# Grouped 3x3 convolution: weights as integers, images as two float32r parts, general path behind a branch

## The chip, the cores and the metric

The kernel runs on one core of one Trainium2 chip. Times are device microseconds (us) of that core. A row of the trace comes from one execution that the hardware profiler recorded; the median comes from three executions without it.

## What is computed

Each image is normalised over groups of four channels, convolved with one of five quantised weight sets, and added to itself. The reference, cut to that:

```python
def _L0_conv_ref(x, U):                 # N = 5, 128 channels in and out, 3x3, padding 1
    beta = jnp.max(U)
    alpha = jnp.min(U)
    s1 = (beta - alpha) / RES_DENOS[0]          # RES_DENOS = (3.0, 5.0)
    v1 = s1 * _ste_floor(U / s1)
    s2 = s1 / RES_DENOS[1]
    v2 = s2 * _ste_floor((U - v1) / s2)
    w = (v1 + v2).reshape(OUT_CH * N, IN_CH, K, K)
    B, C, H, W = x.shape
    xb = x.reshape(B // N, N * C, H, W)
    act = jax.lax.conv_general_dilated(xb, w, ..., feature_group_count=N)
    ...
x = x + _L0_conv_ref(_gn(x), L0_conv_U)  # x: (160, 128, 32, 32) float32; _gn: 32 groups, eps 1e-5
```

A weight is v1 + v2 = s2 * (5 * k1 + k2), where k1 and k2 are the two floors, small integers.

## The kernel before

Channels lie on the 128 partitions. Image i uses set i % 5, and the images are taken set by set: 8 chunks of 4 images for each of 5 sets, 40 chunks, 160 images. SP loads a chunk of 2 MB (`load`, L165) three chunks ahead into one of four `xt` buffers, and ScalarE's queue stores it from the same buffer when its last image is done (L238).

**One image** (`conv`, L204): nine taps, each as two matrix multiplications of 128 x 128 weights with half an image (16 rows of 32, read with a row step of 34 from the padded image `pad`), 18 multiplications into one of three pairs of PSUM banks `pc`. Then VectorE adds `pc` to the image in `xt` (L220): the eviction.

**One chunk's normalisation** (`normalise`, L171) runs while the chunk before it is convolved. VectorE takes statistics of half images (L177), joins them (L178); TensorE averages the means over a group (L181) with `gavg`; VectorE makes `dv` from it in four small steps (L183 to L187); TensorE averages `dv` (L188); VectorE adds eps (L190), GpSimd takes the power -1/2 (L192), and VectorE writes the four normalised images into `pad` (L195). The two small multiplications L181 and L188 stand in TensorE's queue between those of the images.

**One weight set** (`make_weights`, L142): 17 VectorE steps over 128 x 1152 numbers (`floor_div`, L130, twice, and three more), nine transposes on TensorE (L161), three copies to SBUF on ScalarE (L162). Set 0 is made at the start, with the step sizes s1 and s2 from the range of all weights (L91 to L128); a later set is made while the set before it is convolved. All weights and images are float32.

The tile framework sets each engine's order of instructions when the program is built; engines wait for each other by semaphores, and each engine works through its own list in order.

## Time and profile before

| | |
|---|---|
| median of 3 runs | 2566.12 us (2565.94 to 2566.95) |
| profiled execution, first to last instruction (span) | 2564.2 us |
| median less span | 1.9 us |
| TensorE busy with multiplications | 2500.8 us (98%) |
| VectorE busy | 664.1 us (26%) |
| ScalarE busy | 8.5 us |
| GpSimd busy | 52.4 us |
| HBM, read and written | 67 GB/s over the span |

The page counts TensorE's multiplications (PE) and its weight loads (PEld) apart, since they overlap. A float32 multiplication of the program is two records in the trace, each with a weight load of its own: 160 images x 18 multiplications are 2880, and the page has 5760. A record's duration runs until its results are written, so that neighbours overlap: their spacing, and not their duration, is what they cost.

### The profile page before, as it was taken

What the parts mean: (1) busy time and instruction counts of PE and PEld (TensorE: products, weight loads), DVE (VectorE), ACT (ScalarE), POOL (GpSimd) and SP (SyncE); (2) the same over time, 40 slices, a digit from 0 to 9 for tenths busy, and PEclk for the clock granted to TensorE, in tenths of its full rate; (3) what the DMA queues carried; (4) which work ended last, traced back from release to release, by engine and by line L of the source; (5) the groups of instructions that cost most, each with busy time, mean ns of one, the idle gap of its engine ahead of it and who ended that gap; (6) DMA issues with size and microseconds to landing.
All of it is one profiled execution on the core that took longest, in us unless ns stands there. A gap on an engine that the chain in (4) does not pass through costs nothing.

```text
span 2564.2 us, 13452 instructions
## 1 busy us (share of the span) xinstructions
PE 2500.8 (98%) x5965; PEld 1115.1 (43%) x5965; DVE 664.1 (26%) x1113; ACT 8.5 (0%) x16; POOL 52.4 (2%) x59
## 2 busy tenths in 40 slices
PE   1999999999999999999999999999999999999998
PEld 0444444444444444444444444444444444444443
DVE  8542222222522222224222222222222222222110
ACT  0000000000000000000000000000000000000000
POOL 2000000000000000000000000000000000000000
PEclk9999999999999999999999999999999999999999
DMA  4012121111111111111111111111111111111110
GB/s 177 22 64 78 68 78 78 73 66 66 66 66 66 66 66 66 66 66 66 66 66 66 66 66 66 66 66 66 66 66 66 66 66 66 66 66 70 45 45 38
DMA packets 43019, 171.60 MB, mean 67 GB/s; under 512 B 1360, under 2 KB 1360, under 8 KB 42960
## 3 DMA queue, kind: packets, MB, share of 16 engines
q1 hardware_dynamic: 21120, 83.89, 8.8%
q10 hardware_dynamic: 21840, 86.84, 8.2%
q8 instruction: 47, 0.77, 0.1%
q14 instruction: 12, 0.10, 0.0%
HBM read 86.84 MB, written 83.89 MB: 67 GB/s over the span
## 4 chain that ended last, share of the span: by engine, by line
PE 97%; DVE 2%; DMA 1%; ACTq 0%; ACT 0%; issue 0%
PE pc L212 97%; DMA u<-in_L_conv_U_dram 1%; DVE st L177 0%; PE pt L161 0%; PE pg L181 0%; PE pg L188 0%; DVE pad L195 0%; DVE tt L137 0%; DVE tt L138 0%; DVE tt L136 0%; DVE wq L140 0%; DVE tt L139 0%; ACTq L62 0%; DVE nn L134 0%; DVE wq L153 0%; DVE ext L93 0%
## 5 line engine op out<-in xcount | busy, mean ns | idle before, releaser
L212 PE MATMUL pc<-pad,wt 128*128 128x512 f32 x5760 | 2493.6, 593 | 0.0
L212 PEld LDWEIGHTS pc<-pad,wt 128*128 128x128 f32 x5760 | 1084.7, 190 | 1340.1 <-issue 1340.1
L220 DVE TENSOR_TENSOR xt<-xt,pc 128x1024 f32<-128x1024 f32 x160 | 195.4, 1221 | 1785.2 <-PE pc L212 1785.2
L177 DVE BATCH_NORM_STATS2 st<-xt 128x6 f32<-128x512 f32 x320 | 199.8, 663 | 2.8 <-DMA xt<-in_x_dram 2.8
L195 DVE TENSOR_SCALAR pad<-xt,gm,rstd 128x1024 f32<-128x1024 f32 x160 | 119.5, 809 | 46.3 <-POOL rstd L192 46.3
L192 POOL TENSOR_TENSOR rstd<-ve,mhalf 128x4 f32<-128x4 f32 x40 | 42.1, 1053 | 2403.2 <-DVE ve L190 2393.1
L181 PE MATMUL pg<-mv,gavg 128*128 128x4 f32 x80 | 11.8, 218 | 43.1 <-DVE mv L178 43.1
L181 PEld LDWEIGHTS pg<-mv,gavg 128*128 128x128 f32 x80 | 15.4, 196 | 61.4 <-issue 44.1
L178 DVE BATCH_NORM_AGGREGATE mv<-st 128x2 f32<-128x12 f32 x160 | 31.2, 195 | 1.2
L188 PEld LDWEIGHTS pg<-dv,gavg 128*128 128x128 f32 x80 | 15.4, 196 | 26.6 <-DVE dv L187 17.5
L188 PE MATMUL pg<-dv,gavg 128*128 128x4 f32 x80 | 11.8, 218 | 8.2 <-DVE dv L187 8.2
L190 DVE TENSOR_SCALAR ve<-pg 128x4 f32<-128x4 f32 x40 | 6.5, 161 | 39.3 <-PE pg L188 39.3
L140 DVE TENSOR_TENSOR wq<-nn,tt 128x1152 f32<-128x1152 f32 x10 | 13.5, 1353 | 5.2 <-PE pt L161 5.1
L139 DVE TENSOR_TENSOR tt<-tt,nn 128x1152 f32<-128x1152 f32 x10 | 13.5, 1349 | 0.2
L161 PE MATMUL pt<-ident,wq 128*128 128x128 f32 x45 | 9.4, 323 | 3.4 <-DVE wq L153 2.7
L162 ACT COPY wt<-pt 128x512 f32<-128x512 f32 (+1 forms) x15 | 7.2, 478 | 1658.7 <-PE pt L161 1658.7
L161 PEld LDWEIGHTS pt<-ident,wq 128*128 128x128 f32 x45 | 7.0, 200 | 11.5 <-ACT wt L162 6.8
L93 DVE TENSOR_REDUCE ext<-u 128x1 f32<-128x1152 f32 x5 | 6.8, 1353 | 7.0 <-DMA u<-in_L_conv_U_dram 6.8
L87 POOL MEMSET pad<- 128x1156 f32 x8 | 8.1, 1061 | 0.0
L135 DVE TENSOR_SCALAR nn<-nn 128x1152 f32<-128x1152 f32 x10 | 7.5, 753 | 0.1
L153 DVE SCALAR_TENSOR_TENSOR wq<-wq,s,v 128x1152 f32<-128x1152 f32 x5 | 7.1, 1419 | 0.1
L137 DVE SCALAR_TENSOR_TENSOR tt<-nn,s2lo,tt 128x1152 f32<-128x1152 f32 x5 | 7.1, 1419 | 0.1
(44 smaller groups left out, 93.0 us busy)
## 6 DMA issues: line engine op xcount, KB each, us to landing
xt<-in_x_dram SPq DMA_DIRECT2D x40, 2048.0 KB, 7.4
out_dram<-xt ACTq DMA_DIRECT2D x40, 2048.0 KB, 6.4
u<-in_L_conv_U_dram ACTq DMA_DIRECT2D x5, 576.0 KB, 10.2
```

Of the source, the lines that this page charges most:

```text
L87: nc.gpsimd.memset(pad, 0.0)
L139: nc.vector.tensor_tensor(t, t, n, ALU.is_lt)
L140: nc.vector.tensor_sub(k, n, t)
L161: nc.tensor.transpose(pt[:, k, :], wq3[:, :, t0 + k], ident)
L177: nc.vector.bn_stats(st[:, h, :], xt[:, j, h * HALF : (h + 1) * HALF])
L178: nc.vector.bn_aggr(mv[:, j, :], st)
L181: nc.tensor.matmul(pg[:, 0, :], gavg2, mv[:, :, 0], start=True, stop=True)
L188: nc.tensor.matmul(pg[:, 1, :], gavg2, dv, start=True, stop=True)
L192: nc.gpsimd.tensor_tensor(rstd, ve, mhalf, ALU.pow)
L195: nc.vector.tensor_scalar(pad[:, 1 : H + 1, 1 : W + 1], xt[:, j, :].rearrange("p (h w) -> p h w", w=W), gm[:, j : j + 1], rstd[:, j : j + ...
L212: nc.tensor.matmul(pc[:, h, :].rearrange("p (h w) -> p h w", w=W), wt[:, tap, :], pad[:, r0 : r0 + HROWS, kw : kw + W], start=(tap == 0), ...
L220: nc.vector.tensor_add(xj, xj, pc)
```

## The change

The weights that TensorE gets are the integers 5 * k1 + k2 (`make_weights`, L274 of the kernel after), of type float32r. The eviction multiplies by the step size s2 and adds the image in one instruction (L332). An image is normalised into a plain buffer `z` by VectorE (L302), copied to float32r by ScalarE (`hi`, L311), and VectorE writes the rest z - hi as float32r (`lo`, L312). Each tap is then four multiplications: `hi` and `lo`, each for two halves of the image, with the same weights. There are six pairs of padded images in place of eight images, and an image is split two images ahead of its convolution rather than four at a time (`split`). Statistics are as before, in a function of their own (`group_statistics`).

At the end every engine reads a flag (`far`, L165), which was made from the range of the weights at the start, and branches: for weights whose magnitude is over 256 times their range, the whole work is done once more in float32, image by image, in loops (`general_path`, L156). With these inputs the branch skips that.

The diff, cut to its core:

```diff
+MM = mybir.dt.float32r
...
+        self.s2z = col("s2z")
+        nc.vector.tensor_scalar_mul(self.s2z, self.s2, 1.0 / SCALE)
...
+        big, far = col("big"), col("far")
+        self.far = col("fari", I32)
+        nc.vector.tensor_reduce(big, extg, AX.X, ALU.max)
+        nc.vector.scalar_tensor_tensor(far, span, WIDEST, big, ALU.mult, ALU.is_lt)
+        nc.vector.tensor_copy(self.far, far)
...
+def general_path(tc, keep, steps, x, u, out):
...
+    far = nc.values_load(steps.far[0:1, 0:1], min_val=0, max_val=1)
+    with tc.If(far > 0), ExitStack() as ctx:
...
     def make_weights(n):
...
-        nc.vector.scalar_tensor_tensor(wq, wq, s2, v1, ALU.mult, ALU.add)
-
-        wt = const.tile([P, TAPS, C], F32, tag=f"wt{n}", name=f"wt{n}")
...
+        k1, k2, _ = steps.quantise(qpool, us[n], n)
+        nc.vector.scalar_tensor_tensor(k2, k1, 5.0, k2, ALU.mult, ALU.add)
+        wt = const.tile([P, TAPS, C], MM, tag=f"wt{n}", name=f"wt{n}")
...
-        for j in range(NB):
-            pad = pads[(g % 2) * NB + j]
-            nc.vector.tensor_scalar(
-                pad[:, 1 : H + 1, 1 : W + 1],
...
+    def split(g, j, xt, gm, rstd):
+
+        hi, lo = pads[(g * NB + j) % N_PADS]
+        z = zpool.tile([P, H, W], F32, tag="z", name=f"z{g}_{j}")
+        nc.vector.tensor_scalar(
+            z,
...
+        hi_in = hi[:, 1 : H + 1, 1 : W + 1]
+        nc.scalar.copy(hi_in, z)
+        nc.vector.tensor_sub(lo[:, 1 : H + 1, 1 : W + 1], z, hi_in.bitcast(F32))
...
-            for h in range(2):
-                r0 = h * HROWS + kh
-                nc.tensor.matmul(
...
+            for part in range(2):
+                for h in range(2):
+                    r0 = h * HROWS + kh
+                    nc.tensor.matmul(
+                        pc[:, h, :].rearrange("p (h w) -> p h w", w=W),
+                        wt[:, tap, :],
+                        pair[part][:, r0 : r0 + HROWS, kw : kw + W],
...
-        nc.vector.tensor_add(xj, xj, pc)
+        nc.vector.scalar_tensor_tensor(xj, pc, steps.s2z, xj, ALU.mult, ALU.add)
```

**TensorE, around the two small multiplications of a chunk.** Before, they stand in the third image of the chunk ahead; `pc` is an image's result, `pg` theirs:

```order
L212 MATMUL pc_1_376<-pad_107,wt_187 128x512 x18
L181 MATMUL pg_413<-mv_396,gavg 128x4
L212 MATMUL pc_2_430<-pad_109,wt_187 128x512 x3
L188 MATMUL pg_413<-dv_417,gavg 128x4
L212 MATMUL pc_2_430<-pad_109,wt_187 128x512 x15
```

After, in the second image, for a chunk behind the first ones:

```order
L139 MATMUL pg_1167<-mv_1150,gavg 128x4
L324 MATMUL pc_1_1184<-hi_123,wt_210 128x512 x2
L324 MATMUL pc_1_1184<-lo_125,wt_210 128x512 x2
L324 MATMUL pc_1_1184<-hi_123,wt_210 128x512 x2
L324 MATMUL pc_1_1184<-lo_125,wt_210 128x512 x2
L324 MATMUL pc_1_1184<-hi_123,wt_210 128x512 x2
L146 MATMUL pg_1167<-dv_1171,gavg 128x4
```

Between the two stand three multiplications (six records) before, and ten after.

**VectorE, the same place** (behind the eviction whose image ends just ahead of the first small one). Before:

```order
L220 TENSOR_TENSOR xt_257<-xt_257,pc_1_647 128x1024
L183 COPY gm_686<-pg_684 128x4
L185 TENSOR_TENSOR dv_688<-mv_667,gm_686 128x4
L186 TENSOR_TENSOR dv_688<-dv_688 128x4
L187 TENSOR_TENSOR dv_688<-dv_688,mv_667 128x4
L190 TENSOR_SCALAR ve_693<-pg_684 128x4
L195 TENSOR_SCALAR pad_97<-xt_374,gm_686,rstd_695 128x32x32
```

After:

```order
L332 SCALAR_TENSOR_TENSOR xt_507<-pc_0_1110,s2z,xt_507 128x1024
L141 COPY gm_1169<-pg_1167 128x4
L143 TENSOR_TENSOR dv_1171<-mv_1150,gm_1169 128x4
L144 TENSOR_TENSOR dv_1171<-dv_1171 128x4
L145 TENSOR_TENSOR dv_1171<-dv_1171,mv_1150 128x4
L148 TENSOR_SCALAR ve_1176<-pg_1167 128x4
L302 TENSOR_SCALAR z_0_1222<-xt_746,gm_1169,rstd_1178 128x1024
L302 TENSOR_SCALAR z_1_1264<-xt_746,gm_1169,rstd_1178 128x1024
L312 TENSOR_TENSOR lo_113<-z_0_1222,hi_111 128x32x32
L312 TENSOR_TENSOR lo_117<-z_1_1264,hi_115 128x32x32
```

The chain from the eviction to `dv` is the same; the subtractions that make `lo` are added behind it.

**VectorE, the same chain for chunk 2, early in the program, after the change**, where the quantiser of set 2 (`k`, `v`, `u`) stands between its small steps:

```order
L332 SCALAR_TENSOR_TENSOR xt_184<-pc_0_469,s2z,xt_184 128x1024
L141 COPY gm_528<-pg_526 128x4
L93 TENSOR_TENSOR k_2_2271<-nn_2269,tt_2270 128x1152
L143 TENSOR_TENSOR dv_530<-mv_509,gm_528 128x4
L104 TENSOR_SCALAR v_2_2273<-k_2_2271,s_146 128x1152
L144 TENSOR_TENSOR dv_530<-dv_530 128x4
L105 TENSOR_TENSOR u_86<-u_86,v_2_2273 128x1152
L145 TENSOR_TENSOR dv_530<-dv_530,mv_509 128x4
```

There the chain has three large steps more than in the later chunks.

## Rows read from the trace of the kernel before

**Rows 1.** Page: busy time of the engines; and the chain that ended last.

```profile
PE 2500.8 (98%) x5965; PEld 1115.1 (43%) x5965; DVE 664.1 (26%) x1113; ACT 8.5 (0%) x16; POOL 52.4 (2%) x59
...
PE 97%; DVE 2%; DMA 1%; ACTq 0%; ACT 0%; issue 0%
```

**Rows 2.** Groups by line: tiles, shapes, count | busy us, mean ns | idle before.

```profile
L212 PE MATMUL pc<-pad,wt 128*128 128x512 f32 x5760 | 2493.6, 593 | 0.0
L212 PEld LDWEIGHTS pc<-pad,wt 128*128 128x128 f32 x5760 | 1084.7, 190 | 1340.1 <-issue 1340.1
```

**Rows 3.** Pieces of the chain in order of time: start us, us, what.

```profile
279.39 2.68 PE pc L212 x6
282.19 59.35 PE pc L212 x138
341.66 2.68 PE pc L212 x6
```

**Rows 4.** Timeline around one chunk's small multiplications: start us, us, engine, instruction.

```profile
341.38 0.28 PE L181 MATMUL pg<-mv,gavg 128*128 128x4 f32 x2
...
341.52 2.82 PE L212 MATMUL pc<-pad,wt 128*128 128x512 f32 x6
341.58 1.22 DVE L220 TENSOR_TENSOR xt<-xt,pc 128x1024 f32<-128x1024 f32 x1 [9.03 <-PE pc L212]
342.04 0.19 PEld L212 LDWEIGHTS pc<-pad,wt 128*128 128x128 f32 x1 [0.24 <-issue]
...
342.72 0.15 DVE L183 COPY gm<-pg 128x4 f32<-128x4 f32 x1
...
343.30 0.16 DVE L187 TENSOR_TENSOR dv<-dv,mv 128x4 f32<-128x4 f32 x1
```

**Rows 5.** Timeline of TensorE and ScalarE at the transposes of set 1.

```profile
169.28 0.62 PE L161 MATMUL pt<-ident,wq 128*128 128x128 f32 x4
169.28 0.42 PEld L161 LDWEIGHTS pt<-ident,wq 128*128 128x128 f32 x3 [0.24 <-issue]
...
171.33 0.58 ACT L162 COPY wt<-pt 128x512 f32<-128x512 f32 x1 [0.81 <-PE pt L161]
...
172.19 3.17 PE L212 MATMUL pc<-pad,wt 128*128 128x512 f32 x7
172.39 0.27 ACT L162 COPY wt<-pt 128x128 f32<-128x128 f32 x1 [0.47 <-PE pt L161]
```

**Rows 6.** Timeline of the start: first load issued and seen, last quantiser step, images begin.

```profile
0.79 2.77 ACTq L62 DMA_DIRECT2D u<-in_L_conv_U_dram  x5
...
6.41 1.35 DVE L93 TENSOR_REDUCE ext<-u 128x1 f32<-128x1152 f32 x1 [6.41 <-DMA u<-in_L_conv_U_dram]
...
54.91 1.42 DVE L153 SCALAR_TENSOR_TENSOR wq<-wq,s,v 128x1152 f32<-128x1152 f32 x1
...
61.01 29.41 PE L212 MATMUL pc<-pad,wt 128*128 128x512 f32 x67
```

**Rows 7.** Groups by line, VectorE: as rows 2.

```profile
L177 DVE BATCH_NORM_STATS2 st<-xt 128x6 f32<-128x512 f32 x320 | 199.8, 663 | 2.8 <-DMA xt<-in_x_dram 2.8
L220 DVE TENSOR_TENSOR xt<-xt,pc 128x1024 f32<-128x1024 f32 x160 | 195.4, 1221 | 1785.2 <-PE pc L212 1785.2
L195 DVE TENSOR_SCALAR pad<-xt,gm,rstd 128x1024 f32<-128x1024 f32 x160 | 119.5, 809 | 46.3 <-POOL rstd L192 46.3
...
L139 DVE TENSOR_TENSOR tt<-tt,nn 128x1152 f32<-128x1152 f32 x10 | 13.5, 1349 | 0.2
...
L137 DVE SCALAR_TENSOR_TENSOR tt<-nn,s2lo,tt 128x1152 f32<-128x1152 f32 x5 | 7.1, 1419 | 0.1
```

**Rows 8.** Busy us (x instructions) in one chunk's period, then clock, DMA share, GB/s.

```profile
311.00:373.27 62.27, 62.27 (x150) 27.71 (x149) 13.76 (x26) 0.00 (x0) 1.01 (x1) 1.00 0.17 68
```

**Rows 9.** The same, from the last eviction's start to the end.

```profile
2555.54:2564.20 8.66, 0.00 (x0) 0.00 (x0) 1.22 (x1) 0.00 (x0) 0.00 (x0) 0.79 0.59 242
```

## The prediction

> **What bounds the kernel now.** I read the page's busy shares first, then its chain, then the pieces of the chain in order of time. TensorE is busy for 98% of the span and makes up 97% of the chain [rows 1]; nearly all of it is one line, the image multiplications, in 5760 records that never waited (idle before: 0.0) [rows 2]. Their duration, 593 ns, is not what they cost, since they overlap. The chain gives the spacing: 138 records in 59.35 us, 430.07 ns each [rows 3]. [...] Everything else is hidden behind that: a chunk takes 62.27 us, in which VectorE works 13.76 us and ScalarE not at all [rows 8]. The rest of the time is a start of 61.0 us, in which VectorE makes the first weights [rows 6], and an end of 8.7 us with the last eviction and the last store [rows 9].

> The sum for the kernel as it is: start 61.0; 5760 x 0.43007 = 2477.2; small multiplications, 62.27 - 144 x 0.43007 = 0.34 per chunk, times 39 = 13.3; transposes of four later sets, 172.19 - 169.28 = 2.91 us less the four image records between them (1.72) = 1.2 each, 4.8 in all [rows 5]; end 8.7. That is 2565.0 against a span of 2564.2. The median lies 1.9 us above the span, and I carry that along.

> **The change part by part.**

> *Multiplications.* A tap had two multiplications of two records, 4 x 430 = 1720 ns; it gets four float32r ones. Their number, 160 x 36 = 5760, is the number of records before, so the question is what one record costs. No float32r record stands in this trace. From below: one stream of 512 columns is half of 430.07, 215.0 ns; from above: 860 ns, if the type changes nothing. I take one stream plus the whole 3.4 ns, 216.7 ns, because the split into `hi` and `lo` parts with integer weights has a purpose only where a factor is cut to the digits of one stream. 5760 x 0.2167 = 1248.4.

> *Weight loads.* There are as many as before, 5760, each 190 ns long [rows 2], now in half the time. A load starts with the multiplication ahead of it and is over long before that ends (0.19 of 0.43 us [rows 4]); of 216.7 ns it would still leave 27. Pairs of load and multiplication can follow closer than that: the two 4-column ones take 0.14 us together, 70 ns a pair [rows 4], and transposes of 128 columns, where three loads take 0.42 us, are (0.42 - 0.19) / 2 = 115 ns apart [rows 5]. So I count the loads at nothing; the cover is the running multiplication, and without it one costs up to 70 ns, 403 us in all.

> [...]

> *Start.* VectorE's list up to the end of set 0's weights has the same quantiser steps and the same 19 half-image statistics as before. New are six `lo` subtractions, two more `z`, and four tiny steps. A float32 two-input step of 1152 is 1.349 us [rows 7], for 1024 that is 1.22, and the next starts 0.08 before its end (341.58 + 1.22 against 342.72 [rows 4]), so 1.14: six are 6.8. Two `z` at 0.809 - 0.08 are 1.5; the tiny ones 0.5. Sum 8.8, which nothing hides: TensorE starts its images at 61.0 + 8.8 = 69.8. ScalarE's copies (below) lie beside other steps there.

> *Per chunk.* TensorE's period becomes 144 x 0.2167 + 0.34 = 31.5 us. VectorE has its 12.5 (13.76 less the fifth eviction in that window), four `lo` (4.9) and four evictions that multiply too (0.07 more each, by 1.419 against 1.349 [rows 7]): 17.7 of 31.5. ScalarE copies four images: 512 columns take 0.58 and 128 take 0.27 [rows 5], so 1024 about 1.0, 4 us per chunk. Loads and stores move 68 GB/s in this period [rows 8] and would move 135; the end alone has 242 [rows 9]. All covered by TensorE.

> *The wait for `dv`.* The second small multiplication stood six records, 2.6 us, behind the first; now ten, 2.17 us. VectorE's chain to `dv` takes from 341.38 to 343.46, 2.08 us [rows 4], and 0.07 more with the new eviction: 2.15, while the load of the second one wants to start at 0.14 + 9 x 0.2167 = 2.09. It falls short by a little in each chunk; behind the waiting load stand all further image multiplications. From 0 to 0.2 us; I take 0.1 for 35 chunks, 3.5.

> *Early chunks.* The scheduler has put the quantiser of sets 1 to 3 between VectorE's work for chunks 1 to 4, and TensorE now comes past twice as early. Laying VectorE's list end to end with the times above (quantiser steps at 1.33, 1.27 and 0.7): 48 us from the end of set 0's weights, 65.2, to chunk 2's `dv`, 113.3, where TensorE wants it at 69.8 + 5 x 7.8 + 5.8 = 114.6; another 35 to chunk 3's, 148.5, wanted at 147.5; chunk 4's within 1 us. One more such place is at set 3 and 4. I take 4 us, with 0 to 12 as bounds. PSUM's three pairs let evictions be up to two images late, and they are not.

> *Branch.* Five engines read a flag and jump. TensorE, GpSimd and SP do it while the last store (7 us) is under way. No row shows a jump; a trip to memory bounds it, 0.79 to 6.41 [rows 6], 5.6 us, and below it is nothing. I take 1. Transposes and small multiplications stay float32.

> **Sum:** 69.8 + 1248.4 + 13.3 + 4.8 + 3.5 + 4 + 8.7 + 1.9 + 1 = 1355.4, about 1355 us, 47% below 2566.

> **The rivals.**
> *Loads shown.* Loads that a two-stream record covers are not covered by one stream (a load may need the running record's first stream over before it takes effect). For it: the transposes, 115 ns apart where a single stream of 128 columns is 53. Against it: the 27 ns left, and 70 ns pairs. Price 5760 x 0.070 = 403, less the waits (7.5), which then vanish: about 1750.
> *Two streams per float32r record.* A 4-byte operand passes in two streams whatever its name. [...] Then 5760 x 0.43007 = 2477.2 stays, the waits vanish, and start and branch remain: 2577, slower by 0.4%. It decides from a spacing of 428 ns on, where the saving no longer pays for the 9.8 us of start and branch.
> *The type changes nothing.* float32r is run as float32, four streams: 860 ns, 4954 for the multiplications, about 5050. Only the type's name in the program stands against it; no row.

> **How the numbers follow.** The forecast has 0.84: the split is pointless otherwise. Loads shown 0.07, two streams 0.06, nothing changed 0.03. The forecast's own bounds are 1338 (215.0 ns, no waits) and 1372 (waits and branch at their upper ends). No bound stands between a hidden load and a shown one, so I stretch the upper end by a fifth of a load, 14 ns, 80 us, that could show: 1336 to 1430 leaves out the rivals and the forecast's tails. A difference of 0.2% (5 us) is about what can be measured. Faster by more: the first two cases, 0.91. Slower: two streams and nothing changed, 0.09, of which 0.02 falls within 0.2%, as that case lies near its edge.

> **What would show it.** Right: image multiplications in 5760 records at a spacing near 217 ns, about 380 ns long; loads still 190 ns and each beginning with the multiplication ahead; a chunk's period of 31.6 us; TensorE's images starting near 70 us; VectorE busy some 800 us, waiting for TensorE; waits of TensorE for `dv` of some us in chunks 2 to 4 and 11 and of 0.1 elsewhere. Wrong: a spacing near 285 (loads shown), 430 (two streams), or twice as many records; a chunk's period set by VectorE or ScalarE; more than 6 us between the last store's landing and the end.

## The result and the profile after

The changed kernel takes 1505.62 us (median of 4 runs, 1504.94 to 1506.34) against 2566.53 us before: a ratio of 0.5866, with a 95% interval of 0.5858 to 0.5875. It takes 41% less time. The prediction had the direction, but its 1355 us and the upper end of its range, 1430, are too low. The profiled execution spans 1504.2 us.

The page, as [rows 1]: TensorE still makes the chain, 95% of it; VectorE has 846 us in place of 664, ScalarE 170 in place of 8.5.

```profile
PE 1430.8 (95%) x5965; PEld 1119.2 (74%) x5965; DVE 846.3 (56%) x1277; ACT 169.7 (11%) x176; POOL 57.1 (4%) x63
...
PE 95%; DVE 3%; DMA 1%; ACTq 0%; ACT 0%; issue 0%
```

The groups by line (tiles, shapes, count | busy us, mean ns | idle before), as [rows 2]. The number of records is the same, 5760, so a float32r multiplication is one record; it lasts 408 ns in place of 593. Loads still take 190 ns, and multiplications wait for nothing.

```profile
L324 PE MATMUL pc<-hi,wt 128*128 128x512 f32 x2880 | 940.8, 408 | 0.0
L324 PE MATMUL pc<-lo,wt 128*128 128x512 f32 x2880 | 940.4, 408 | 0.0
L324 PEld LDWEIGHTS pc<-lo,wt 128*128 128x128 f32 x2880 | 544.8, 190 | 150.8 <-issue 0.2
```

The pieces of the chain (start us, us, what), as [rows 3]; the first is the first chunk of all, the others one later chunk. 134 records take 32.72 us: 244.2 ns each, where 430.07 was the spacing before and 216.7 the forecast.

```profile
69.46 44.60 PE pc L324 x177
...
934.13 0.12 PE pg L139 x2
934.25 2.55 PE pc L324 x10
936.80 0.12 PE pg L146 x2
936.92 32.72 PE pc L324 x134
```

The busy time of the engines (PE, PEld, DVE, ACT, POOL, with instructions), then clock, DMA share and GB/s, for one chunk's period and for the end, as [rows 8, 9]. VectorE and ScalarE work 18.36 and 4.10 of 35.51 us, so nothing but TensorE sets the period.

```profile
224.44:259.95 35.51, 35.51 (x150) 27.78 (x150) 18.36 (x29) 4.10 (x4) 1.01 (x1) 1.00 0.30 122
1494.23:1504.20 9.97, 0.00 (x0) 0.00 (x0) 1.28 (x1) 0.00 (x0) 0.00 (x0) 0.60 0.53 215
```

The timeline around a chunk's two small multiplications, as [rows 4]: `dv` ends at 1363.36, the load of the second small multiplication begins at 1363.64. TensorE no longer waits there.

```profile
1361.42 1.28 DVE L332 SCALAR_TENSOR_TENSOR xt<-pc,s2z,xt 128x1024 f32<-128x1024 f32 x1 [7.49 <-PE pc L324]
...
1363.20 0.16 DVE L145 TENSOR_TENSOR dv<-dv,mv 128x4 f32<-128x4 f32 x1
...
1363.64 0.43 PEld L146 LDWEIGHTS pg<-dv,gavg 128*128 128x128 f32 x2
1363.88 0.28 PE L146 MATMUL pg<-dv,gavg 128*128 128x4 f32 x2
```

So one term holds the miss, 27.5 ns in each of 5760 multiplications, 158 us; waits that did not come take 7.5 us of it back. The experiments ask where these nanoseconds are. Two places of the same trace narrow it before any run. One is the last image, behind the eviction of the image before it, where TensorE is the only engine at work (busy times, clock, DMA share and GB/s below) and 24 records, from 1487.21 to 1493.06, take 5.85 us, 243.8 ns each. So it is not contention with other engines.

```profile
1486.80:1494.20 7.40, 7.39 (x31) 5.42 (x29) 0.00 (x0) 0.00 (x0) 0.00 (x0) 1.00 0.01 2
```

```profile
1487.21 0.65 PE L324 MATMUL pc<-hi,wt 128*128 128x512 f32 x2
...
1493.06 0.65 PE L324 MATMUL pc<-hi,wt 128*128 128x512 f32 x2
```

The other is the first image, ahead of 72.25 us, where the records come in pairs 0.85 us apart:

```profile
69.69 1.05 PE L324 MATMUL pc<-hi,wt 128*128 128x512 f32 x2
...
70.54 1.05 PE L324 MATMUL pc<-lo,wt 128*128 128x512 f32 x2
```

That is 426.5 ns each, 0.833 ns a column. The busy-time view prints a granted clock of 1.00 here too, but the trace's first entry of a granted clock is at 72.88 us, where the spacing falls to 244; so the lower level is read from the spacing. The same 0.83 ns a column stands in e4 below at a granted clock of 0.50. My estimate from these two places is half as much at 1.00: 213.3 ns for 512 columns by themselves, 0.417 each; the 0.417 and 106.7 ns in the expectations agree with it. What is missing seems to show only when the columns pass faster than 0.833 ns each; e4 and e17 below test that.

### The profile page after: what moved, and what is told of

Read it like the earlier page. It is cut to its first block, busy times and chain, and to the rows that moved or that the text cites. A ratio compares the mean times of both kernels' runs of the same rounds, so it can differ in the third digit from the quotient of the medians.

```text
span 1504.2 us, 14064 instructions
## 1 busy us (share of the span) xinstructions
PE 1430.8 (95%) x5965; PEld 1119.2 (74%) x5965; DVE 846.3 (56%) x1277; ACT 169.7 (11%) x176; POOL 57.1 (4%) x63
## 4 chain that ended last, share of the span: by engine, by line
PE 95%; DVE 3%; DMA 1%; ACTq 0%; ACT 0%; issue 0%
PE pc L324 94%; DMA u<-in_L_conv_U_dram 1%; DVE st L135 1%; DVE lo L312 0%; PE pt L284 0%; PE pg L139 0%; PE pg L146 0%; DVE z L302 0%; DVE tt L89 0%; DVE tt L91 0%; DVE tt L90 0%; DVE tt L92 0%; DVE k L93 0%; ACTq L252 0%; DVE nn L87 0%; DVE nn L88 0%
## 5 line engine op out<-in xcount | busy, mean ns | idle before, releaser
L324 PE MATMUL pc<-hi,wt 128*128 128x512 f32 x2880 | 940.8, 408 | 0.0
L324 PE MATMUL pc<-lo,wt 128*128 128x512 f32 x2880 | 940.4, 408 | 0.0
L324 PEld LDWEIGHTS pc<-lo,wt 128*128 128x128 f32 x2880 | 544.8, 190 | 150.8 <-issue 0.2
L324 PEld LDWEIGHTS pc<-hi,wt 128*128 128x128 f32 x2880 | 543.6, 190 | 149.7
L332 DVE SCALAR_TENSOR_TENSOR xt<-pc,s2z,xt 128x1024 f32<-128x1024 f32 x160 | 204.8, 1280 | 543.7 <-PE pc L324 543.7
L311 ACT CAST hi<-z 128x1024 fp32r<-128x1024 f32 x160 | 161.2, 1053 | 1236.5 <-DVE z L302 1219.9
L312 DVE TENSOR_TENSOR lo<-z,hi 128x1024 fp32r<-128x1024 f32 x160 | 189.2, 1223 | 16.6 <-ACT hi L311 16.6
L302 DVE TENSOR_SCALAR z<-xt,gm,rstd 128x1024 f32<-128x1024 f32 x160 | 123.2, 810 | 44.6 <-POOL rstd L150 44.6
L284 PE MATMUL pt<-ident,k 128*128 128x128 f32 x45 | 8.7, 308 | 28.3 <-DVE k L277 27.7
L93 DVE TENSOR_TENSOR k<-nn,tt 128x1152 f32<-128x1152 f32 x10 | 13.5, 1355 | 2.7 <-PE pt L284 2.6
L39 DVE TENSOR_REDUCE ext<-u 128x1 f32<-128x1152 f32 x5 | 6.8, 1353 | 7.1 <-DMA u<-in_L_conv_U_dram 7.1
```

The lines of the kernel that those rows point to most:

```text
L284: nc.tensor.transpose(pt[:, k, :], k3[:, :, t0 + k], ident)
L302: nc.vector.tensor_scalar(z, xt[:, j, :].rearrange("p (h w) -> p h w", w=W), gm[:, j : j + 1], rstd[:, j : j + 1], ALU.subtract, ALU.mult,)
L311: nc.scalar.copy(hi_in, z)
L312: nc.vector.tensor_sub(lo[:, 1 : H + 1, 1 : W + 1], z, hi_in.bitcast(F32))
L324: nc.tensor.matmul(pc[:, h, :].rearrange("p (h w) -> p h w", w=W), wt[:, tap, :], pair[part][:, r0 : r0 + HROWS, kw : kw + W], start=(tap ...
L332: nc.vector.scalar_tensor_tensor(xj, pc, steps.s2z, xj, ALU.mult, ALU.add)
```

## Experiments

The measure is the spacing: a piece of 134 multiplications on the chain, divided by 134 (fewer where it says so), to hold against 244.2 ns. A time with a range behind it is the median of four executions; the others come from one.

### Is it the load of the weights?

`e1_m64` loads and uses half of the weight columns.

```diff
-                        pc[:, h, :].rearrange("p (h w) -> p h w", w=W),
-                        wt[:, tap, :],
+                        pc[:64, h, :].rearrange("p (h w) -> p h w", w=W),
+                        wt[:, tap, :64],
```

> Weights of 64 columns in place of 128 (the results of output channels 64 to 127 are left out); the moving columns stay. The changed kernel spaces its image multiplications 244.2 ns apart (134 in 32.72 us) where 216.7 was forecast. Theory A, part of each weight load is shown, in proportion to its columns: half of the 27.5 ns goes, spacing about 230 ns, time about 1505 - 5760 x 0.0137 = 1426 us. Theory B, a column of four bytes takes 0.477 ns in place of 0.417: spacing stays 244, time 1505 us. Theory C, each of the 16 rows of the moving operand costs 1.7 ns more: spacing stays 244, 1505 us.

1497.61 us. Groups by line and the chain:

```profile
L324 PEld LDWEIGHTS pc<-lo,wt 128*64 128x64 f32 x2880 | 390.1, 136 | 300.0 <-issue 0.6
```

```profile
931.28 32.62 PE pc L324 x134
```

A load is 54 ns shorter, the spacing 0.8 (243.4). The load is not what shows; my rival *Loads shown* falls, and with it the fifth of a load by which I had stretched the range.

### Is it the way in which the images are read?

`e2_contig` reads 512 neighbouring numbers in place of 16 rows of 32; `e3_rows16` reads 32 rows of 16; `e4_n256` reads 8 rows of 32, half the columns.

```diff
-                        pair[part][:, r0 : r0 + HROWS, kw : kw + W],
+                        pair[part].rearrange("p h w -> p (h w)")[:, r0 * 34 + kw : r0 * 34 + kw + HALF],   # e2
+                        pair[part][:, kh : kh + H, h * 16 + kw : h * 16 + kw + 16],                       # e3
+                        pair[part][:, r0 : r0 + 8, kw : kw + W],                                          # e4
```

> The moving operand is 512 neighbouring numbers of the padded image in place of 16 rows of 32 (so the convolution of other pixels is summed). Theory A (load shown): spacing stays 244 ns, 1505 us. Theory B (slower column): 244 ns, 1505 us. Theory C (rows): the 27.5 ns go, 217 ns, about 1505 - 5760 x 0.0275 + some us of waits for dv = 1350 us.

> The moving operand is 32 rows of 16 columns (the left or the right half of an image) in place of 16 rows of 32; all is computed, with the pixels of the result in another order. Theories A and B: spacing stays 244 ns, 1505 us. Theory C (each row costs 1.7 ns): 216.7 + 32 x 1.72 = 272 ns, about 1505 + 5760 x 0.0275 = 1663 us.

> Each multiplication streams 256 columns (8 rows of 32) in place of 512, and as many multiplications: the lower half of each half image is left out. Theory A (27.5 ns of each load shown): 106.7 + 3.4 + 27.5 = 138 ns. Theory B (column at 0.477 ns): 122 ns. Theory C (8 rows at 1.7 ns): 106.7 + 3.4 + 13.8 = 124 ns. Times by 5760 x the spacing and the 99 us beside it: 894, 802 and 813 us, if VectorE, with 17 us of work in a chunk's 17.9 to 20.2, does not begin to bound; the spacing is read inside an image.

1442.22, 1627.27 and 842.65 us. The longest undisturbed pieces of the three chains:

```profile
251.35 31.22 PE pc L324 x134
```

```profile
352.83 35.56 PE pc L324 x134
```

```profile
175.38 14.39 PE pc L324 x115
```

233.0, 265.4 and 125.1 ns. More and shorter rows cost time, one long row gives 11 ns back, but 16 remain above the forecast. With half the columns other engines set part of the time, so only the spacing counts for e4.

### Is it the type?

`e5_fp16` is the changed kernel with one line changed (and two casts that go with it): weights and both parts of the images are float16.

```diff
-MM = mybir.dt.float32r
+MM = mybir.dt.float16
```

> The type alone: weights and both image parts in float16 in place of float32r (11 digits a part; the integers fit), all else as in the changed kernel. Theory D, the 27.5 ns above one stream are the reading of 4-byte operands: half the bytes, spacing 216.7 ns, 1505 - 158 = 1347 us, and up to 10 us of waits for dv back, since the second small multiplication then stands 2.17 us behind the first: 1347 to 1357. Theory E, they belong to the multiplication's shape (16 rows, strided) whatever the type: 244 ns, 1505 us. Theory A (load shown) says 244 to 230 ns, since a 2-byte load may be shorter, 1425 to 1505 us.

1372.28 us (1371.66 to 1372.92), 0.5348 of before (0.5339 to 0.5357). A piece of its timeline:

```profile
925.00 0.59 PE L324 MATMUL pc<-lo,wt 128*128 128x512 f16 x2
925.43 0.62 PE L324 MATMUL pc<-hi,wt 128*128 128x512 f16 x2
925.89 0.62 PE L324 MATMUL pc<-lo,wt 128*128 128x512 f16 x2
926.35 0.59 PE L324 MATMUL pc<-hi,wt 128*128 128x512 f16 x2
```

```profile
598.62 29.61 PE pc L324 x134
```

Pairs follow at 0.43 us (216 ns each), but two of every six at 0.46 (230): those of the middle taps, whose rows start 2 bytes off a multiple of 4. With these the mean is 221.0. Two bytes per number take the surplus away. (The loads of the weights are shorter here too, 98 ns in place of 190, but e1 has shown that this gains next to nothing.) Where a row starts matters for float16 too.

### Where do the rows start?

`e6_aligned` reads 512 neighbouring float32r numbers from a multiple of 64 bytes; `e7_alrows` 16 rows of 32, each from such a multiple; `e9_al256` is e6 with 256 columns, set up when e6 had given 231.3 ns, 18.0 above the estimate of 213.3 for its 512 columns; `e12_al_m32` is e6 with 32 weight columns.

```diff
+            flat = const.tile([P, 1168], MM, tag=f"{part}{i}", name=f"{part}{i}")
...
-                        pair[part][:, r0 : r0 + HROWS, kw : kw + W],
+                        pair[part][:, 16 * (tap + 9 * h) : 16 * (tap + 9 * h) + HALF],                    # e6
+                        pair[part][:, 16 * (tap + 9 * h) : 16 * (tap + 9 * h) + 768].rearrange("p (r c) -> p r c", c=48)[:, :, :32],   # e7
```

> float32r, 512 neighbouring numbers whose first stands at a multiple of 64 bytes (other pixels are summed); the neighbouring numbers of the second experiment began at multiples of 4 bytes and took 233.1 ns. Theory D1, what remained there (16 ns over 216.7) is the first and last piece of a line of 64 bytes read in vain or twice: 217 ns, 1350 us. Theory D2, a 4-byte column simply takes 0.44 ns when it is streamed once: stays at 233 ns, 1442 us.

> float32r, 16 rows of 32 as in the changed kernel, but each row begins at a multiple of 64 bytes (row step 48 numbers in place of 34; other pixels are summed). If the rows cost by the lines that they touch (3 lines for a row of 128 bytes off its line, 2 on it): spacing as for neighbouring numbers, 233 ns or, if alignment helps there too, 217; 1442 or 1350 us. If they cost by their number: stays at 244 ns, 1505 us.

> [...] Theory K, the 18 ns are a constant per multiplication: 106.7 + 18 = 124.7 ns. Theory L, they go with the columns (0.452 ns each): 115.7 ns. Time about 800 us either way, with VectorE near its bound; the spacing is read inside an image.

> float32r, 512 neighbouring numbers from a multiple of 64 bytes as in the sixth experiment (231.3 ns), with weights of 32 columns in place of 128 (three quarters of the output channels are left out). If a part of the load is what remains above 216.7: up to three quarters of 14.6 ns go, 220 ns, 1367 us. If the columns themselves take 0.44 ns: 231 ns, 1430 us.

1430.80, 1458.64, 810.09 and 1437.13 us. Their chains, in this order:

```profile
316.86 30.99 PE pc L327 x134
```

```profile
321.40 31.64 PE pc L327 x134
```

```profile
700.18 14.49 PE pc L327 x122
```

```profile
318.51 31.20 PE pc L327 x134
```

231.3, 236.1, 118.8 and 232.8 ns. A quarter of the weight columns gains nothing at all (it is 1.5 ns longer), so the load is out for good. From 256 to 512 columns the spacing grows by 112.5 ns, 0.4395 per column, where the estimate of 213.3 for 512 has 0.4166: of the 18.0 ns that e6 lies above 213.3, 11.7 grow with the columns, between the two theories of e9. At this point I read e6 and e7 as "row starts off 64 bytes cost 8 ns", which fell later (e18).

### Values, reading or type?

Three edits of e6: `e13_zero` multiplies zeros, `e14_same` reads one and the same number 512 times, `e15_step2` every other of 1024 numbers.

```diff
-        nc.scalar.copy(hi_in, z)
-        nc.vector.tensor_sub(lo[:, 1 : H + 1, 1 : W + 1], z, hi_in.bitcast(F32))
+        nc.scalar.mul(hi_in, z, 0.0)                                                                      # e13
+        nc.vector.tensor_sub(lo[:, 1 : H + 1, 1 : W + 1], hi_in.bitcast(F32), hi_in.bitcast(F32))         # e13
...
-                        pair[part][:, 16 * (tap + 9 * h) : 16 * (tap + 9 * h) + HALF],
+                        pair[part][:, 16 * (tap + 9 * h) : 16 * (tap + 9 * h) + 1].to_broadcast([P, HALF]),   # e14
+                        pair[part][:, 16 * tap : 16 * tap + 2 * HALF : 2],                                # e15
```

> As in e6_aligned (512 neighbouring float32r numbers from a multiple of 64 bytes), but all images that TensorE reads are zero: the convolution is left out of the output. Theory R (what a float32r column takes beyond a cycle lies in reading four bytes per column): the values do not matter, 231.3 ns stay, 1431 us. Theory P (it lies in the work on the values: multiplying zeros is held back less): near 217 ns, about 1350 us.

> As in e6_aligned, but all 512 columns of a multiplication are one and the same number of each partition (step 0): other pixels are summed than in the convolution. Theory R, if reading is by stretches of memory: one stretch serves all columns, near 217 ns, 1347 us. Theory T (the type alone sets the 0.44 ns of a column, wherever it is read from): 231.3 ns stay, 1431 us.

> As in e6_aligned, but the 512 columns are every other one of 1024 numbers (step 2, 8 bytes): other pixels are summed than in the convolution. Theory R: twice the stretch of memory is read per column; if that sets the pace, up to twice 0.44 ns, 450 ns a multiplication, 2690 us; some of it in any case, over 240 ns. Theory T: 231.3 ns stay, 1431 us.

1430.80, 1354.22 and 2710.21 us. The chains:

```profile
316.79 30.99 PE pc L327 x134
```

```profile
307.15 29.03 PE pc L327 x134
```

```profile
615.37 60.81 PE pc L327 x134
```

231.3, 216.6 and 453.8 ns. The values change nothing. Reading one number brings the forecast's spacing (216.7) and its total (1355) almost exactly; reading twice the stretch doubles the time. float32r passes 512 columns in 216.6 ns, 0.42 each, as I had assumed; what no run got in that time is 512 different four-byte numbers.

### What is counted: pieces of 16 bytes

The 512 neighbours of e6 are 128 pieces of 16 bytes, the 1024 of e15 256. Their difference, 222.5 ns for 128 pieces, is 1.74 ns a piece, and 8.8 ns per multiplication are left. Three more edits of e6 vary the pieces alone: `e16_quads` reads four of every eight numbers, each four in one piece; `e17_quads_off` the same shifted by 8 bytes, each four in two pieces; `e18_rows36` is e7 with rows that start at multiples of 16, most not of 64.

```diff
+                        pair[part][:, 16 * tap : 16 * tap + 1024].rearrange("p (r c) -> p r c", c=8)[:, :, :4],    # e16
+                        pair[part][:, 16 * tap : 16 * tap + 1024].rearrange("p (r c) -> p r c", c=8)[:, :, 2:6],   # e17
+                        pair[part][:, 16 * (tap + 9 * h) : 16 * (tap + 9 * h) + 576].rearrange("p (r c) -> p r c", c=36)[:, :, :32],   # e18
```

> As in e6_aligned, but the 512 columns are four of every eight of 1024 numbers, each four from a multiple of 16 bytes: other pixels are summed than in the convolution. Theory B (what is read are pieces of 16 bytes, 1.74 ns each and 8.8 ns per multiplication, worked out from the 128 pieces of e6_aligned in 231.3 ns and the 256 of e15_step2 in 453.8): 128 pieces, 231 ns, 1431 us, somewhat more if a row has a cost of its own (e7_alrows has 0.3 ns for each of 16 rows; 128 rows here, up to 270 ns, 1650 us). Theory S (pieces of 64 bytes, or the whole stretch): as e15_step2, 454 ns, 2710 us.

> As in e16_quads, but each four starts 8 bytes behind a multiple of 16, so that it lies in two pieces of 16 bytes: other pixels are summed than in the convolution. Theory B: 256 pieces, 454 ns, 2710 us. Theory S: no difference to e16_quads, whatever that gives.

> As in e7_alrows (16 rows of 32), but with a row step of 36 numbers, so that the rows start at multiples of 16 bytes and most not of 64: other pixels are summed than in the convolution. Theory B: 128 pieces as in e7_alrows, 231 ns and its 4.8 for the rows, 236 ns, 1459 us. Theory S (row starts off 64 bytes cost the 8.1 ns between e7_alrows and the changed kernel): 244 ns, 1506 us.

1443.25, 2710.45 and 1454.43 us. The chains:

```profile
318.66 31.27 PE pc L327 x134
```

```profile
615.60 60.82 PE pc L327 x134
```

```profile
320.71 31.56 PE pc L327 x134
```

233.4, 453.9 and 235.5 ns. A shift by 8 bytes alone nearly doubles the time, because each four numbers then lie in two pieces; 64-byte starts do not matter (235.5 against e7's 236.1). With 8.8 + 1.74 per piece, fitted to e6 and e15 alone, the other float32r runs come out so (pieces counted from the addresses, mean of the nine taps):

| kernel | pieces | 8.8 + 1.74 x pieces | measured |
|---|---|---|---|
| changed kernel, 16 rows of 32, step 34 | 136.1 | 245.6 | 244.2 |
| e2, neighbours | 128.7 | 232.7 | 233.0 |
| e3, 32 rows of 16 | 149.3 | 268.6 | 265.4 |
| e4, 8 rows of 32 | 68.1 | 127.3 | 125.1 |
| e7, e18, 16 rows in 128 pieces | 128 | 231.5 | 236.1, 235.5 |
| e9, 256 neighbours | 64 | 120.2 | 118.8 |
| e16 | 128 | 231.5 | 233.4 |
| e17 | 256 | 454.2 | 453.9 |

All within 5 ns, as means over the nine taps. For e3 that is in part luck: its middle taps touch 160 pieces (287 ns by the formula), the others 144 (259), and the trace has the same spacing for both. Four records of an outer tap stand between 353.30 and 354.36, four of the middle one between 354.36 and 355.41:

```profile
353.30 0.69 PE L324 MATMUL pc<-hi,wt 128*128 128x512 f32 x2
...
354.36 0.69 PE L324 MATMUL pc<-hi,wt 128*128 128x512 f32 x2
...
355.41 0.69 PE L324 MATMUL pc<-hi,wt 128*128 128x512 f32 x2
```

So the size of a piece is shown by e16 and e17, while the price of short rows is a fit of means only.

With two numbers from each piece e15 takes 453.8 ns; with four e6 takes 231.3, still 14.7 above e14.

The traces also show how columns and pieces go together. In e4 a stretch in mid-run has a granted clock of 0.50; pairs of its records of 256 columns are 0.43 us apart there, 213 ns each, 0.83 a column. At 1.00 they take 125.1, 18 more than half of that. So the surplus is gone at the lower clock.

```profile
120.20:123.40 3.20, 3.20 (x15) 3.20 (x16) 3.20 (x6) 1.41 (x2) 0.00 (x0) 0.50 1.02 401
```

```profile
121.12 0.63 PE L324 MATMUL pc<-lo,wt 128*128 128x256 f32 x2
121.55 0.63 PE L324 MATMUL pc<-hi,wt 128*128 128x256 f32 x2
```

In e17, where the pieces (454.2 ns by the formula) take longer than the columns at either clock (426.5 and, by the estimate, 213.3), the clock does not matter. Its first entry of a granted clock is at 72.33 us; pairs are 0.91 us apart, 453 ns each, ahead of that (where the changed kernel has 426.5) and behind it:

```profile
70.20 1.09 PE L327 MATMUL pc<-hi,wt 128*128 128x512 f32 x2
71.11 1.08 PE L327 MATMUL pc<-lo,wt 128*128 128x512 f32 x2
...
72.92 1.09 PE L327 MATMUL pc<-lo,wt 128*128 128x512 f32 x2
73.83 1.09 PE L327 MATMUL pc<-hi,wt 128*128 128x512 f32 x2
```

So in these runs the columns go with TensorE's clock (213 ns for 256 at 0.50 in e4) and the reading does not (453 ns in e17 at both levels), and the later of the two sets the spacing.

### Versions that get the forecast's spacing

`e8_fp16_shift` is e5 with copies of both parts that are shifted by one column (`hs` by ScalarE, `ls` by GpSimd), from which the middle taps read, so that all rows start at multiples of 4 bytes. `e11_fp16_border` is e8, but GpSimd clears only the borders of the 24 padded images.

```diff
+        nc.scalar.copy(hs[:, 1 : H + 1, :W], z)
+        nc.gpsimd.tensor_copy(ls[:, 1 : H + 1, :W], lo_in)
...
-                        pair[part][:, r0 : r0 + HROWS, kw : kw + W],
+                        pair[part][:, r0 : r0 + HROWS, kw : kw + W]
+                        if kw != 1
+                        else pair[2 + part][:, r0 : r0 + HROWS, :W],
...
-            nc.gpsimd.memset(pad, 0.0)                                               # e11
+            nc.gpsimd.memset(pad[:, 0 : H + 2 : H + 1, :], 0.0)                      # e11
+            if part in ("hi", "lo"):                                                 # e11
+                nc.gpsimd.memset(pad[:, 1 : H + 1, 0 : W + 2 : W + 1], 0.0)          # e11
```

> float16 as in the fifth experiment, and copies of both image parts shifted by one column, made by ScalarE and GpSimd, from which the middle column of taps is read, so that every row of every tap begins at a multiple of 4 bytes. In the fifth experiment two pairs in six were 0.46 us apart and four 0.43. Theory G, the slow ones are the middle taps, whose rows begin between two multiples of 4 bytes: all pairs at 0.43, spacing 216 ns, 5760 / 3 x 0.015 = 29 us gained, 1343 us, up to 10 us more if the start waits for the added copies. Theory H, the slow pairs belong to something else (ScalarE's or VectorE's writes, the change of weights): they stay, 1372 us or more.

> The eighth experiment, where GpSimd clears only the borders of the padded buffers in place of whole buffers: 24 clearings of 1.07 us each stood ahead of the reduction over all partitions, which ran at 32.8 us there, and TensorE's images began at 83.5 us against 69.4 in the fifth experiment. If the clearings are why the start grew: the reduction at about 21 us, images from about 70 to 74 us, 1363 - 10 to 13 = 1350 to 1353 us. If the copies on ScalarE and GpSimd hold the start: no change, 1363 us.

e8: 1362.83 us (1362.75 to 1363.87), 0.5311 of before (0.5302 to 0.532). The spacing is 216.6, but its start had grown, TensorE's images beginning at 83.5 us behind the last transpose (69.4 in e5). GpSimd's timeline has 24 clearings of 1.07 us each, and behind them the step that joins the range of the weights over the partitions, from which the step sizes are made. It stands idle for another 5.92 us before that step, until VectorE has done statistics that the framework had put into VectorE's list meanwhile.

```profile
572.68 29.02 PE pc L327 x134
```

```profile
25.77 1.08 POOL L268 MEMSET ls<- 128x1156 f16 x1
32.77 0.37 POOL L44 PARTITION_ALL_REDUCE extg<-ext  x1 [5.92 <-DVE st L135]
```

e11: 1350.64 us (1350.03 to 1352.53), 0.5264 of before (0.5255 to 0.5273), the fastest kernel here. The same step in its timeline, and its chain:

```profile
21.10 0.37 POOL L44 PARTITION_ALL_REDUCE extg<-ext  x1 [14.46 <-DVE ext L42]
```

```profile
939.50 29.02 PE pc L329 x134
```

216.6 ns again. The step now waits for its input `ext` alone and comes 11.7 us earlier; TensorE's images begin at 60.9 us, 22.6 earlier, but 12.2 us are what the median keeps: from 68.9 to 110.0 us the chain runs through VectorE's list (evictions, statistics, the quantiser of the next set, and `lo`, 2.3 us of it at 79.5 and again at 86.0), which the earlier images now wait for. This is the time that I had forecast for float32r, reached with half the bytes.

### The branch

`e10_nobranch` leaves out the general path and the branch to it.

> The changed kernel without the general path and its branch (the flag is still made). The stretch from the last eviction's start to the end was 8.66 us before and is 9.97 in the changed kernel. If the branch is the difference: 8.7 us, and about 1.3 us (0.1%) off the time. If the end belongs to the store: 10 us and no change. No theory of the spacing is touched: 244 ns.

1503.95 us (1503.32 to 1504.33). The busy times from the last eviction's start to the end:

```profile
1492.85:1501.60 8.75, 0.00 (x0) 0.00 (x0) 1.28 (x1) 0.00 (x0) 0.00 (x0) 0.71 0.58 240
```

8.75 us, as before [rows 9], against 9.97 with the branch: it costs 1.2 us in the profile and 1.7 by the medians.

## Why the prediction missed

The terms of its sum, beside what the trace of the changed kernel has:

| term | forecast, us | measured, us |
|---|---|---|
| start, until TensorE's images | 69.8 | 69.46 |
| 5760 multiplications | 1248.4 (216.7 ns) | 1406.6 (244.2 ns) |
| small multiplications | 13.3 | 39 x (35.51 - 144 x 0.2442) = 13.4 |
| transposes of four sets | 4.8 | 4 x (33.77 - 32.72, 134 records with and without a set's) = 4.2 |
| waits for `dv`, every chunk and early ones | 3.5 + 4 | none between images |
| end, with the branch | 8.7 + 1 | 9.97 |

The failed step is the multiplication term: "I take one stream plus the whole 3.4 ns, 216.7 ns". No run shows these 3.4 ns, and that a record of before is two streams was my assumption; what the runs showed in their place is 216.6 ns where one number is read 512 times (e14), and 244.2 for the images. So the stream was right, and the term left out that its numbers have to be read. In the kernel before, a record took 430 ns for 512 columns, 0.84 each [rows 3], and the reading of the same rows, 244 ns in the changed kernel, would be hidden in that. No run shows it apart there, but the stretch of e4 at a granted clock of 0.50, 213 ns for 256 columns, shows the same cover for float32r. Halving the time of a column uncovered it. I had named the cover of the weight loads and priced its loss; of the other operand I had asked nothing, although the rows of before say only that its reading fits into 430 ns. Bounded by the nearest rows from both sides, the term lay between 215 and 430 ns, and the stretch of the range by "a fifth of a load" had no row behind it: e1 shows that the load is not what is late. (The 80 us of that stretch, put on the bound of 1372, would also give 1452, and on the forecast 1435, not the 1430 that stands there; 1506 lies beyond each.) Of the 27.5 ns, 14.7 remain for 512 neighbouring numbers in 128 pieces (e6); the other 13 come with the rows.

*Loads at nothing* was right. Halving them gave 0.8 ns (e1), and e14 has a load of 190 ns for each multiplication at a spacing of 216.6:

```profile
L327 PEld LDWEIGHTS pc<-lo,wt 128*128 128x128 f32 x2880 | 543.4, 190 | 75.6 <-issue 0.2
```

So the rival by which each load shows does not hold here.

The other steps:

- *Start*: right within 0.4 us, with six subtractions, two `z` and the small steps.
- *Chunk*: VectorE 18.36 us (17.7 forecast), ScalarE 4.10 (4), 122 GB/s, all covered. The period is 35.51 us in place of 31.5, by the multiplications alone.
- *Waits for `dv`*: none, and for the reason of the large miss: ten records now take 2.44 us and not 2.17, longer than VectorE's chain. In e5, where they take 2.23, the loads of the small multiplications wait for `dv` in each of 40 chunks, 18.1 us in all, of which 7.4 lie in the start; the multiplications themselves wait 9.8 us, 7.2 of it in the start.
- *Early chunks*: no wait in the stream of images. At the forecast's spacing, in e14, TensorE waits 3.2 us for `dv` behind the start, where 7.5 were forecast. The two that the changed kernel's trace has lie ahead of the first image:

```profile
PE pg L146 <- DVE dv L145: 7.2, 2, 4.9
```

- *Branch*: 1 us forecast, 1.2 to 1.7 measured (e10).
- *Two streams* (430 ns) and *the type changes nothing* (860 ns) are refuted by the spacing.

With 27.5 x 5760 = 158 us added and the waits' 7.5 taken off, the sum is 1506, the measured time.

Not settled: 16 rows of 32 in 128 pieces (e7, e18) take 4 to 5 ns more than one row (e6), and the 8 pieces more of the changed kernel only 1.1 ns each beyond that, so that rows and pieces do not simply add; nor do they tap by tap in e3. Why float16 rows off 4 bytes take 230 ns and not 216 was not followed further; by pieces they hardly differ from the others (about 68 in each tap).

## What to carry over

When a change halves what an engine spends on each element, price again everything that the longer time had covered: the reading of each operand as well as the loads, and bound it by the old time where no row shows it. For a stream into TensorE count both the columns (0.42 ns each for float32r in e14 and float16 in e11) and the 16-byte pieces that its rows touch (1.74 ns each here, within 5 ns a multiplication as a mean over the taps); the later one sets the spacing. Two-byte types (216.6 ns in e11) and rows that begin with a piece (235.5 in e18) shorten it from 244.2. A small experiment that reads one number over and over tells reading from computing at once.
